# A mark ahead of GpSimd's register loads, and two loads of results issued one expert tile further ahead

## The chip, the cores and the metric

The kernel runs on one core of a Trainium2 chip. The metric is the device time of one execution in microseconds (us), as the median of several runs. A profile of one execution shows what each engine did: TensorE (PE, its weight loads PEld), VectorE (DVE), ScalarE (ACT), GpSimd (POOL) and SyncE (SP). An engine's instructions pass through its sequencer (PEq, SPq, POOLq and so on in the profile), which waits on semaphores, loads registers, takes branches and issues DMAs.

## What is computed

Four batches of 512 tokens of width 512 pass through a gated linear cross attention over a context of 1024 rows, and then through a mixture of eight experts, of which each token uses two. All is float32.

```python
def _L0_ffn_ref(x, Wr, We, be):
    logits = jnp.einsum('bsd,de->bse', x, Wr)
    w, sel = jax.lax.top_k(logits, K_TOP)
    w = jax.nn.softmax(w, axis=-1)
    gate = jnp.einsum('bsk,bske->bse', w, jax.nn.one_hot(sel, E, dtype=w.dtype))
    out = jnp.zeros(x.shape[:2] + (We.shape[2],), dtype=x.dtype)
    for e in range(E):
        out = out + gate[..., e:e + 1] * (jnp.einsum('bsd,df->bsf', x, We[e]) + be[e])
    return out
x = x + _L0_xattn_ref(_layernorm(x, axis=-1), ctx_2048, ...)
x = x + _L0_ffn_ref(_layernorm(x, axis=-1), L0_ffn_Wr, L0_ffn_We, L0_ffn_be)
return x
```

The change lies in the last stage, the mixture of experts.

## The kernel before

**Stages.** For each batch in turn the kernel forms keys and values of the context, the attention of the batch's tokens, and the router's choice of two experts for each token. `dispatch` (line 519) then scatters each token's normalized row, from GpSimd, into a DRAM buffer `stream`, which has one region for each expert. Rows of one expert are later read back in tiles of 128.

**Expert tiles.** At most 39 tiles (ALLT) of 128 rows can arise. The first 17 (EARLY) hold rows of the first three batches alone and run in between the last batch's attention. The other 22 (LATE) come after the last dispatch. 18 of these (SURE) always run; the remaining four stand in a branch, `tc.If(many > SURE)` of line 1012, which is taken only if the streams hold more tiles. In the profiled execution it isn't: there are 35 scatters of results, 17 + 18. Each engine takes this branch at its own time, and an engine that skips the body brings the semaphores of the body's work up to date.

**One expert tile** (`run`, line 677) has four parts. `rows` loads 128 rows from `stream` on SyncE (line 704), five tiles ahead. `turned` turns them on DVE (line 721), three tiles ahead. `expert` multiplies by the expert's weights on TensorE, adds the bias on DVE into y (line 753), and scatters y from GpSimd with an indirect DMA into a DRAM buffer `result` (line 757), where each choice of each token has one row.

**Token tiles.** The 16 token tiles of 128 tokens are put together again as their results become complete: `fetch` (line 810) loads both results of each token of a tile, 512 KB, from `result`; `add` (line 834) weights them and adds them to the attention's output, two instructions on DVE (line 840); `store` (line 849) writes the output, 256 KB. For token tiles 0 to 13 this is spread over the steps of the late loop (`for j in range(-5, SURE)`, line 995): `begins` (line 867) has for each token tile the step after which it is loaded. The add comes three steps later and the store one step after the add, on GpSimd's queue; from begins of SURE - 4 (14) on, adds and stores fall to step SURE, which is traced after the branch, with the stores on ScalarE's queue. Token tiles 14 and 15 are loaded after the branch, on SyncE's and ScalarE's queues (lines 1022 and 1023). They wait for all scatters of results.

**Which results a load waits for.** READ (line 46) has five groups of token tiles: 0 to 3, 4 to 7, 8 and 9, 10 and 11, 12 and 13. Each comes with the number of expert tiles that hold all of the group's results if the tokens spread well; a load waits for the scatters of these expert tiles alone. Whether the assumption holds is computed (`where_to_read`, line 800); if not, the group's load reads other rows, and the token tiles are done again at the end. The row to read from is therefore a number computed on the chip, and the first `fetch` of a group loads it into a register of GpSimd's sequencer (`nc.values_load`, line 820). Tiles 12 and 13 need the scatters of all early tiles and of late tiles 0 to 15.

**The order of instructions on an engine** is made by the framework's scheduler, from dependences and a model of the work; it may move an instruction past others that the program has ahead of it. `tc.keep_in_program_order(ins)` ties an instruction behind the one that was traced just before it on the same engine. `mark` (line 455) is a memset of one cell on GpSimd, tied in this way. It is traced ahead of each scatter of results, ahead of each load of results and ahead of each store, and these are tied as well: a mark stays behind whatever was traced before it, and the DMA behind the mark. `values_load` isn't tied. So after a group's first `fetch` the order in the program is

```
mark, scatter of the expert tile, register load, mark, load, mark, load or store ...
```

in which the mark behind the register load is tied to the register load, and not to the scatter. `tc.issue_after(latest["y"].ins)` around each step's additional work ties DVE's instructions of it behind the last y, and no other engine's.

In the late loop, the program order on GpSimd is, for step j: the scatter of late tile j (for j below 0 that of early tile 17 + j), then what `at_step[j]` holds, loads ahead of stores. Behind step 17 come the register loads for the two branches (line 1006) and the branch.

Of the kernel before, what the change touches and what calls it, by code (L numbers as in the profile page):

```python
# [39 lines left out]
SURE = LATE - 4  # L40
# [13 lines left out]
def xattn_moe_kernel(  # L54
# [388 lines left out]
    def behind(dma, puts, why):  # L443

        for put in puts:
            tc.add_manual_dep(
                dma.ins,
                put.ins.name,
                mybir.DependencyInfo(mybir.DependencyClass.Sync, mybir.DependencyReason.DATA),
                reason=why,  # L450
            )
# [3 lines left out]
    def mark():  # L455

        tc.keep_in_program_order(nc.gpsimd.memset(marked, 0.0))
# [352 lines left out]
    def fetch(t, tiles, queue, group=None):  # L810

        pool, tag = homes[t // 2 % len(homes)]
        if t not in fetched:
            pair = pool.tile([P, 2, 2, F], F32, tag=tag, name=f"y_{t}")
            fetched[t], fetched[t + 1] = pair[:, 0], pair[:, 1]
        if group is None:
            src = flat[:, t]
        else:
            if group not in rows_of:
                rows_of[group] = nc.values_load(  # L820
                    spots[0:1, group : group + 1], [queue.engine], min_val=0, max_val=NOWHERE,
                    skip_runtime_bounds_check_because="one of two constants",
                )
            row = rows_of[group] + (t - READ[group][0]) * 2 * P
            src = result[ds(row, 2 * P), :].rearrange("(p i) f -> p i f", i=2)
        mark()
        load = queue.dma_start(out=fetched[t], in_=src)
        behind(load, written["result"][:tiles], "results of the tokens")
        for put in written["result"][tiles:]:
            tc.declare_no_dep(load.ins, put.ins, reason=read_again)  # L830
        tc.keep_in_program_order(load)
        read_back.append(load)
# [31 lines left out]
    def plan(step, *what):  # L864
        at_step.setdefault(min(step, SURE), []).append(what)

    begins = (-3, -2, -1, 0, 5, 6, 7, 8, 10, 11, 14, 15, SURE - 1, SURE - 1)
    for g, (lo, hi, most) in enumerate(READ):
        for t in range(lo, hi):
            plan(begins[t], fetch, t, most, nc.gpsimd, g)  # L870
# [151 lines left out]
    for t in range(half, B * NT):  # L1022
        fetch(t, ALLT, queues[t % 2])
# [5 lines left out]
    with tc.If(again > 0):  # L1029
        for t in range(half):  # L1030
            fetch(t, ALLT, nc.sync)
            add(t, gates_end)
            store(t, nc.sync)
# [43 lines left out]
```

## Time and profile before

| what | us |
|---|---|
| median of 3 runs | 621.65 |
| lowest and highest of these | 619.83, 622.51 |
| the profiled execution, its time | 622.61 |
| its span, from first to last instruction | 621.0 |
| TensorE busy | 588.5 (95% of the span) |
| DVE busy | 271.0 (44%) |
| GpSimd busy | 100.6 (16%) |
| scatter of results, line 757, 35 of them | 35.8 in all, 1.02 each |
| issue of a load of results, line 827, GpSimd, 14 of them | 0.546 to 0.605 each |
| such a load, 512 KB, from issue to landing | 4.6 to 6.8 |
| issue of a store, line 851, GpSimd, 10 of them | 0.547 to 0.598 each |
| register load of line 820, 5 of them | 0.302, 0.311, 0.707 (least, median, most) |
| mark (memset of one cell) | 0.09 |

The granted clock of TensorE is 0.983 over the span. Moved bytes and the DMA engines' share in stretches at the end of the kernel:

| stretch, us | DMA share | GB/s |
|---|---|---|
| 570 to 580 | 0.94 | 272 |
| 580 to 590 | 0.93 | 288 |
| 590 to 600 | 0.62 | 185 |
| 600 to 607.3 | 0.63 | 218 |
| 607.3 to 613.7 | 0.81 | 229 |
| 613.7 to 621 | 0.42 | 159 |

In rows of the timeline the first number is the start in us from the start of the span, the second the length in us, then engine, line, operation and tiles (out<-in), and in brackets how long the engine was idle before and what ended this. `<-issue` stands for time in which the engine waited for nothing that the profile shows. The length of a DMA's row on GpSimd is that of its issue, not of the transfer.

### The profile page before, as it was taken

What the parts mean: (1) busy time and instruction counts of PE and PEld (TensorE: products, weight loads), DVE (VectorE), ACT (ScalarE), POOL (GpSimd) and SP (SyncE); (2) the same over time, 40 slices, a digit from 0 to 9 for tenths busy, and PEclk for the clock granted to TensorE, in tenths of its full rate; (3) what the DMA queues carried; (4) which work ended last, traced back from release to release, by engine and by line L of the source; (5) the groups of instructions that cost most, each with busy time, mean ns of one, the idle gap of its engine ahead of it and who ended that gap; (6) DMA issues with size and microseconds to landing.
All of it is one profiled execution on the core that took longest, in us unless ns stands there. A gap on an engine that the chain in (4) does not pass through costs nothing. (4 is left out here: it accounts for less than half of the span.)

```text
span 621.0 us, 6578 instructions
## 1 busy us (share of the span) xinstructions
PE 588.5 (95%) x1908; PEld 286.3 (46%) x1908; DVE 271.0 (44%) x668; ACT 115.2 (19%) x180; POOL 100.6 (16%) x274
## 2 busy tenths in 40 slices
PE   7999999999999999999999999999999999999940
PEld 3555543454565335446643454565434554443410
DVE  2222243216215341351454226127874569475663
ACT  1322222112322221142222211322210100000000
POOL 4100000000002200000050000002311227455540
PEclk9999999999999999999999999999999999999985
DMA  8648920682686227527530660933344444889965
GB/s 317 191 158 301 293 81 2 167 240 69 164 248 184 81 86 237 153 85 221 186 137 1 203 204 0 327 130 137 116 114 119 96 119 177 262 243 259 296 219 173
DMA packets 68597, 105.55 MB, mean 170 GB/s; under 512 B 11981, under 2 KB 30413, under 8 KB 68176
## 3 DMA queue, kind: packets, MB, share of 16 engines
q1 hardware_dynamic: 58944, 76.24, 41.7%
q0 software_dynamic: 8176, 26.78, 12.1%
q10 hardware_dynamic: 1440, 2.10, 1.1%
q8 instruction: 16, 0.26, 0.2%
q14 instruction: 21, 0.17, 0.1%
HBM read 45.93 MB, written 59.94 MB: 170 GB/s over the span
## 5 line engine op out<-in xcount | busy, mean ns | idle before, releaser
L91 PE MATMUL pk<-wkv_sb,cT 128*128 128x512 f32 x256 | 118.6, 607 | 4.4 <-DMA cT<-in_cT_dram 4.4
L91 PE MATMUL pv<-wkv_sb,cT 128*128 128x512 f32 x256 | 115.2, 593 | 0.0
L221 DVE TENSOR_SCALAR ex<-pk 128x512 f32<-128x512 f32 x32 | 22.0, 688 | 148.3 <-PE pk L91 148.3
L91 PEld LDWEIGHTS pv<-wkv_sb,cT 128*128 128x128 f32 x256 | 48.4, 190 | 62.3 <-issue 59.3
L91 PEld LDWEIGHTS pk<-wkv_sb,cT 128*128 128x128 f32 x256 | 47.7, 194 | 57.8 <-issue 49.9
L91 PE MATMUL pe<-we_sb,xgT 128*128 x144 | 62.8, 595 | 0.6 <-DVE xgT L721 0.6
L91 PE MATMUL pe<-we_sb,turned_rows 128*128 x136 | 60.3, 597 | 0.7 <-DVE turned_rows L721 0.7
L278 POOL MEMSET v<- 128x4 f32 x32 | 3.3, 105 | 345.3 <-PE kvs L91 282.3
L91 PE MATMUL pg<-xT,wg_sb 128*128 128x512 f32 x128 | 56.7, 596 | 0.0
L91 PE MATMUL pq<-xT,wq_sb 128*128 128x512 f32 x128 | 56.6, 596 | 0.0
L91 PE MATMUL po<-wo_sb,aT 128*128 128x512 f32 x128 | 55.6, 592 | 0.0
L222 ACT ACTIVATE ex<-ex 128x512 f32<-128x512 f32 x48 | 30.2, 630 | 136.2 <-DVE ex L221 126.6
L757 POOL DMA_INDIRECT result<-y,to x35 | 35.8, 1023 | 93.7 <-DVE y L753 88.4
L91 PEld LDWEIGHTS pe<-we_sb,xgT 128*128 128x128 f32 x144 | 27.0, 190 | 36.3 <-issue 29.9
L91 PEld LDWEIGHTS pe<-we_sb,turned_rows 128*128 128x128 f32 x136 | 25.3, 190 | 32.4 <-issue 29.5
L563 POOL DMA_INDIRECT stream<-row,slot x32 | 31.9, 996 | 50.3 <-DVE cmp L591 22.5
L91 PEld LDWEIGHTS kvs<-v,k 128*128 128x128 f32 x256 | 33.3, 191 | 13.4 <-issue 13.4
L91 PEld LDWEIGHTS pg<-xT,wg_sb 128*128 128x128 f32 x128 | 24.0, 190 | 32.1 <-issue 32.1
L91 PEld LDWEIGHTS po<-wo_sb,aT 128*128 128x128 f32 x128 | 24.1, 190 | 29.2 <-issue 28.7
L91 PEld LDWEIGHTS pq<-xT,wq_sb 128*128 128x128 f32 x128 | 23.8, 190 | 27.3 <-issue 27.3
L91 PE MATMUL kvs<-v,k 128*128 128x129 f32 x256 | 34.0, 275 | 0.0
L223 DVE SCALAR_TENSOR_TENSOR k<-pk,ex 128x512 f32<-128x512 f32 x32 | 22.1, 690 | 19.5 <-ACT ex L222 19.5
(175 smaller groups left out, 465.1 us busy)
## 6 DMA issues: line engine op xcount, KB each, us to landing
stream<-empty SPq DMA_DIRECT2D x24, 1028.0 KB, 8.1
stream<-empty SPq DMA_DIRECT2D x8, 1285.0 KB, 6.8
xg<-stream SPq DMA_DIRECT2D x140, 64.0 KB, 2.7
we_sb<-in_we_dram SPq DMA_DIRECT2D x32, 256.0 KB, 5.5
cT<-in_cT_dram SPq DMA_DIRECT2D x31, 256.0 KB, 3.1
y<-result POOLq DMA_DIRECT2D x14, 512.0 KB, 5.5
x<-in_x_dram SPq DMA_DIRECT2D x16, 256.0 KB, 6.6
out_dram<-y POOLq DMA_DIRECT2D x10, 256.0 KB, 4.6
```

The costliest lines, as they stand in the source:

```text
L91: tc.keep_in_program_order(nc.tensor.matmul(**operands))
L221: nc.vector.tensor_scalar(ex, src, 0.0, None, ALU.min)
L222: nc.scalar.activation(ex, ex, AF.Exp)
L223: nc.vector.scalar_tensor_tensor(dst, src, 0.0, ex, ALU.max, ALU.add)
L278: nc.gpsimd.memset(v[:, :, P : P + 1], 1.0)
L563: put = nc.gpsimd.indirect_dma_start(out=stream, out_offset=bass.IndirectOffsetOnAxis(ap=slots[i][:, t, :], axis=0), in_=rows[t], in_offse ...
L757: put = nc.gpsimd.indirect_dma_start(out=result, out_offset=bass.IndirectOffsetOnAxis(ap=home_i, axis=0), in_=y, in_offset=None, bounds_ch ...
```

## The change

Two lines. In `fetch`, a mark is traced ahead of the register load of a group. It applies to the five groups, whose first loads stand in steps -3, 5, 10, 14 and, for tiles 12 and 13, the step of the second edit. In `begins`, token tiles 12 and 13 move from step SURE - 1 (17) to step SURE - 2 (16).

```diff
             if group not in rows_of:
+                mark()
                 rows_of[group] = nc.values_load(
                     spots[0:1, group : group + 1], [queue.engine], min_val=0, max_val=NOWHERE,
                     skip_runtime_bounds_check_because="one of two constants",
...
-    begins = (-3, -2, -1, 0, 5, 6, 7, 8, 10, 11, 14, 15, SURE - 1, SURE - 1)
+    begins = (-3, -2, -1, 0, 5, 6, 7, 8, 10, 11, 14, 15, SURE - 2, SURE - 2)
```

The new mark is tied behind the scatter of the step's expert tile, since this is what was traced just before it on GpSimd. Adds and stores of token tiles 12 and 13 stay at step SURE, behind the branch.

## The prediction

> **What bounds the kernel now.** I read the page first, then the chain that ended last, then GpSimd's rows of the last 30 us, and at the end DVE's rows and the branch's own rows. TensorE is busy 95% of the span, but the change touches only GpSimd's queue, so what counts is where that queue decides something. The chain shows one such place, the end:
>
> ```profile
> 590.10 0.56 POOL y L827
> 590.66 0.08 POOL marked L457
> 590.74 1.28 issue
> 592.02 11.38 DMA out_dram<-y
> 603.41 0.09 POOLq L1012
> ...
> 604.72 2.33 DMA result<-y,to
> ...
> 607.30 6.38 DMA y<-result
> ```
>
> Each row is start, length and what it was. TensorE's last matmul ends at 597.3. From there the kernel waits for one scatter, that of late tile 17: it starts at 604.72, lands 2.33 later, and only then do SyncE and ScalarE load the results of token tiles 14 and 15 (6.38). The adds and stores behind that end the span at 621.0. GpSimd's rows say why the scatter is so late:
>
> ```profile
> 592.88 1.02 POOL L757 DMA_INDIRECT result<-y,to  x1 [0.23 <-issue]
> 595.60 1.02 POOL L757 DMA_INDIRECT result<-y,to  x1 [1.70 <-DVE y L753]
> ...
> 598.18 1.02 POOL L757 DMA_INDIRECT result<-y,to  x1 [0.27 <-DVEq L1012]
> 599.18 0.23 POOL L457 MEMSET marked<- 1x1 f32 x2
> 600.06 0.56 POOL L827 DMA_DIRECT2D y<-result  x1 [0.64 <-issue]
> 600.62 0.09 POOL L457 MEMSET marked<- 1x1 f32 x1
> 600.71 0.55 POOL L827 DMA_DIRECT2D y<-result  x1
> 604.72 1.03 POOL L757 DMA_INDIRECT result<-y,to  x1 [3.46 <-issue]
> ```
>
> The indirect DMAs are the scatters of tiles 14, 15, 16 and 17, the direct ones the loads of token tiles 12 and 13. In the program tile 17's scatter stands ahead of both loads; here it comes after them, and after more. Its input was long there, and GpSimd did something else in between:
>
> ```profile
> 597.35 0.69 DVE L753 TENSOR_TENSOR y<-pe,be_sb 128x512 f32<-128x512 f32 x1 [1.21 <-PE pe L91]
> 598.38 0.18 DVE L1003 COPY gates_end<-gates 128x32 f32<-128x32 f32 x1 [0.34 <-DVEq L1012]
> ```
>
> ```profile
> L1012 POOLq COMPARE_BRANCH   x1: 53/53/53, 601.1 to 601.1; - x1
> L1012 POOLq INC_SWDGE_SEM  x1: 2002/2002/2002, 601.5 to 601.5; - x1
> ```
>
> Tile 17's y is done at 598.04. GpSimd takes the branch of line 1012 at 601.1 and spends 2.00 us in a semaphore update that belongs to the skipped body, and the scatter follows. So it slipped past the register loads, the two loads and the whole branch. The same happened to the copy into gates_end on DVE, which the program also has ahead of the branch. The slips have a rule: a scatter stays in place only where the next mark is traced right behind it. Where a register load is, the next mark is tied to that load. Five scatters had such a place (early tile 14, late tiles 5, 10, 14, 17), and all five slipped.
>
> **The change, part by part.** Late tile j's scatter is s(j), token tile t's load f(t).
>
> *Five more marks.* Each memset is 0.09 us. They tie s to the line: s, new mark, register load, mark, f. That the second mark stays behind the first follows from both writing one cell. So in four places s goes ahead of f, and f waits for DVE's y.
>
> - Group 0: y of early tile 14 ends at 529.01. Scatters start 0.28 after their y (585.97 to 586.25), so at 529.3 instead of 531.43. f(0): 529.3 + 1.02 scatter + 0.24 for two marks + 0.64 to issue (as at 589.23 to 590.10) = 531.2 instead of 530.54. It lands by 536 and is added at 542.83.
> - Group 1: y(5) ends at 557.31; s(5) 557.6 instead of 559.52; f(4) 559.5 instead of 558.65. It landed at 564.1, now 565.0; added at 570.67.
> - Group 2: y(10) ends at 576.56; s(10) 576.8 instead of 577.11; f(8) 578.7 instead of 575.63. With 4.6 to 6.8 to land (the row of these loads) 583.3 to 585.5; added at 590.20.
> - Group 3: y(14) ends at 592.32; s(14) 592.6 instead of 592.88; f(10) 594.5 instead of 590.10, behind it the store of tile 8 at 595.1, then s(15) at 594.5 + 1.48 (f, store, scatter as at 575.63, 576.26, 577.11) = 596.0 instead of 595.60. **Term: +0.4 us for everything behind it on GpSimd.** f(10) lands near 599.8, its add stood at 599.60: the cover is used up, 0.2 us late. That is absorbed, since the adds of tiles 10 to 13 end near 608 and DVE then idles until 613.7 for tile 14.
>
> In the first three I cost the later load at nothing: 7, 5.7 and 4.7 us lie between landing and add. Without that cover DVE would stand by the delay, 0.7 to 3.1 us, and y and TensorE behind it.
>
> *Tiles 12 and 13 a step ahead.* They need the scatters up to s(15), in both orders. Their order on GpSimd is s(16), mark, register load, mark, f(12), mark, f(13): the very order of the trace of before, with one mark of another origin. So f(12) and f(13) do not come earlier, but 0.4 later: 600.44 and 601.09, landing at 605.0 and 606.3. The mark of tile 17 now stands behind f(13), at 601.6.
>
> *What becomes of s(17)?* The shift has taken the last register load of fetch from behind it. What is traced next are the register loads of line 1006 and the branch, and neither has a mark in front. So s(17) is as free as before to slip past the branch. Nothing in the trace shows this order, so both ends are to be priced.
>
> Below: it slips again. f(13), branch, 2.00 us update, s(17), all 0.4 later: 605.1, loads at 607.7, the span 621.0 + 0.4 = 621.4. Above: it stays ahead of the branch. s(17) starts 0.31 after tile 17's mark (576.80 to 577.11), at 601.95. Landing 2.33 later is 604.3. But the final loads wait for the skipped body's semaphores too: ScalarE's and SyncE's waits moved on only when that update was over. From the end of f(13) (601.26) to its end (603.50) was 2.24; behind s(17) that makes 601.95 + 1.03 + 2.24 = 605.2, and with the 0.26 between the last release and the load (607.04 to 607.30) 605.5 instead of 607.30, a gain of 1.8.
>
> I take the first. In group 2 GpSimd ran through four DMAs (s(9), a store, f(8), a store) and a further mark before the scheduler saw y(10) ready; between y(16) and y(17) there are now only three and the mark. And gates_end on DVE shows that the branch was placed before y(17) was over. **Sum: +0.4 us** (bounds 0, if y(15) hides the delay, and +0.9, with a register load of 0.71, the longest of line 820, in place of 0.31).
>
> The profiled execution took 622.61 with a span of 621.0; the median is 621.65 (619.83 to 622.51), 0.96 lower. I put the difference on the median: 621.65 + 0.4 = 622.05, said as 622.1.
>
> The Trainium skill ("TensorE: Matmul & The Clock Gate", the table at its head) calls GpSimd's queue strictly first in, first out. This speaks against the change: a load that is tied behind a scatter can't pass it while the scatter waits for DVE. The rows agree, no f starts while an s ahead of it waits; if loads could pass, the +0.4 would be 0.
>
> The skill also gives a register load a floor of about 600 ns ("DMA: Bandwidth & Descriptors", Latency and other measured facts). The rows of line 820 have 302 at least and 311 in the middle, so the measurement decides. By the page the two loads of groups 3 and 4 would add some 0.6 us (an estimate), a median of 622.6.
>
> **The rivals.**
>
> *s(17) stays ahead of the branch.* For it: tile 17's mark is now behind f(13), and the branch's own marks come behind that one; if y(17) is ready by then, the scatter is first in the program. Against: five slips of five. Time: 621.65 - 1.8 = 619.8. If the 2.00 us update overlaps the scatter, the loads start at 604.3 + 0.26, a gain of 2.7; and if they land in the 5.5 of the other loads instead of 6.38, because two of the four stores beside them come later, 3.6: 618.1.
>
> *Loads collide with tile rows (the slower side).* f(8) and the store behind it, 768 KB, move 3.1 us, into the stretch 580 to 590 where the DMA share is 0.93 at 288 GB/s and three weight loads already idled 0.75, 0.55 and 0.66 us for late rows instead of the usual 0.24, 1.24 too long together. 768 KB at 288 GB/s are 2.7 us. All of it on the rows' path gives 0.4 + 2.7 = 3.1, 624.8. It decides from the point where those three gaps grow by more than the 1.8 that the rival above could save, and shows as slower only if all of it arrives. Against it: the sum of the DMA work is unchanged, and the same bytes leave the stretch before. The mirror image is worth the 1.24 of the gaps.
>
> *The marks do not hold.* If two writes of one cell are no tie for the scheduler, s(16) slips behind f(12) and f(13), which wait for s(15)'s landing (598.24). GpSimd's work is the same, only permuted, up to the branch: 621.7.
>
> **How the numbers follow.** Slips again 0.47, stays ahead 0.33, collision 0.13, marks do not hold 0.07. A measurement of this kernel tells about 0.5% from no change, 3.1 us: below 618.5 or above 624.8. Under 618.5 lie the better half of the second case and a little of a mirrored collision: 0.20. Above 624.8 lie the worse part of the collision and what I have not seen: 0.13. Within: 0.67. The forecast's own range is 621.6 to 622.6. The range of 8 in 10 runs from the second case's end to just below the collision at full price: 618.1 to 624.5.
>
> **What would show it.** Right: in GpSimd's rows s(17) still follows the branch and the 2.00 us update, near 605; s(5), s(10), s(14) stand ahead of f(4), f(8), f(10); f(10) near 594.5; the adds of tile 10 wait a little. Wrong: two scatters with only the two loads between them and the branch behind, the final loads near 605.5; or DVE idle for y<-result ahead of an add before 598, or TensorE's last matmul off 597.3 by over 1 us.

## The result, and the profile after

The changed kernel takes 622.57 us (median of 20 runs, 621.02 to 624.17), the kernel before in the same runs 621.11 (20 runs, 619.41 to 624.33). The ratio is 1.0028, with a 95% interval of 1.0018 to 1.0037: slower by 0.3%, 1.5 to 1.7 us, inside the 0.5% that were called no change. Measured again on another chip it was 623.30 against 622.47, 1.0024 [1.0006, 1.0043].

The profiled execution of the changed kernel took 621.79, with a span of 620.2 and a granted clock of 0.982. That one execution is shorter than the profiled one of before (span 621.0), because late tile 17's y was ready at 596.32 and not at 598.04; what follows y is longer. So places in the two traces are compared below by their distance from an event ahead of all that changed at the end: the end of y(14), 592.33 before and 590.60 after.

GpSimd's rows of the changed kernel (start, length, engine, line, operation, tiles, and in brackets the idle time before with what ended it):

```profile
590.89 1.01 POOL L757 DMA_INDIRECT result<-y,to  x1 [3.86 <-DVE y L753]
...
592.73 0.59 POOL L828 DMA_DIRECT2D y<-result  x1 [0.61 <-issue]
...
593.33 0.58 POOL L852 DMA_DIRECT2D out_dram<-y  x1
...
594.27 1.02 POOL L757 DMA_INDIRECT result<-y,to  x1 [0.30 <-DVE y L753]
...
595.32 0.55 POOL L828 DMA_DIRECT2D y<-result  x1
...
596.83 1.02 POOL L757 DMA_INDIRECT result<-y,to  x1 [0.29 <-issue]
...
599.16 0.56 POOL L828 DMA_DIRECT2D y<-result  x1 [1.10 <-DMA result<-y,to]
...
599.82 0.55 POOL L828 DMA_DIRECT2D y<-result  x1
...
600.70 1.02 POOL L757 DMA_INDIRECT result<-y,to  x1 [0.25 <-issue]
```

The direct loads are f(10), f(11), f(12), f(13), the scatters s(14) to s(17). Two things are to be seen. The scatter of tile 14 now stands ahead of f(10), so f(10) and the store behind it come just ahead of s(15); and f(12) waits 1.10 for a scatter's landing, where in the trace of before it had waited for nothing shown. And s(17), the last row, comes straight behind f(13), ahead of the branch: it is no longer behind the 2.0 us semaphore update. That update follows it (rows of the branch's line, with least, median and most ns and the start):

```profile
L1013 POOLq INC_SWDGE_SEM  x1: 2017/2017/2017, 601.8 to 601.8; - x1
```

All the same the final loads came no sooner. The rows of the scatters' line in a window that holds s(17) alone give its time to land:

```profile
L757 POOL DMA_INDIRECT result<-y,to x1: 1023/1023/1023, 600.7 to 600.7; - x1
...
DMA to landing us min/median/max: 5.4/5.4/5.4
```

5.41 us, where it took 2.33 before. It lands at 606.11. The update ended at 603.85, and the rows of the final loads on their queues show that SyncE then stood in one event wait of 2253 ns, from 603.88 to 606.13, right up to that landing:

```profile
L828 SPq EVENT_SEMAPHORE  x4: 28/28/2253, 603.9 to 606.3; - x4
```

So the sum at the end, all from rows: s(17) starts 12.39 behind the end of y(14) before, 10.09 after, 2.30 earlier; it lands 3.08 slower; the final loads stand at 14.93 before and 15.72 after, 0.79 later. The end of the span moves from 28.69 to 29.61.

Two rows of DVE answer to the copy into gates_end that had slipped behind the branch:

```profile
596.24 0.20 DVE L1004 COPY gates_end<-gates 128x32 f32<-128x32 f32 x1
597.32 0.75 DVE L841 SCALAR_TENSOR_TENSOR y<-y,gates_end,x 128x512 f32<-128x512 f32 x1 [0.88 <-DMA y<-result]
```

It stays ahead of the branch now too, and the first add of token tile 10 waits 0.88 for f(10).

### The profile page after: what moved, and what is told of

Its sections match the earlier page's. It is cut to its first block, busy times and chain, and to the rows that moved or that the text cites. A ratio compares the mean times of both kernels' runs of the same rounds, so it can differ in the third digit from the quotient of the medians.

```text
span 620.2 us, 6584 instructions
## 1 busy us (share of the span) xinstructions
PE 587.0 (95%) x1908; PEld 286.1 (46%) x1908; DVE 271.1 (44%) x668; ACT 115.2 (19%) x180; POOL 100.6 (16%) x279
## 5 line engine op out<-in xcount | busy, mean ns | idle before, releaser
L91 PEld LDWEIGHTS kvs<-v,k 128*128 128x128 f32 x256 | 33.3, 191 | 13.4 <-issue 13.4
L753 DVE TENSOR_TENSOR y<-pe,be_sb 128x512 f32<-128x512 f32 x35 | 24.0, 687 | 15.8 <-PE pe L91 13.3
```

The costliest lines, as they stand in the source:

```text
L91: tc.keep_in_program_order(nc.tensor.matmul(**operands))
L753: latest["y"] = nc.vector.tensor_tensor(y, pe, be_sb[:, ds(no, 1), :].rearrange("p o f -> p (o f)"), ALU.add)
```

## The experiments

Twelve runs were made, on several chips and each beside the kernel before on the same chip: nine new kernels, one of them twice, and both kernels of the change once more. Three theories stood against each other. **Queue:** the loss arises in GpSimd's queue at the end, from group 3's mark (f(10) ahead of s(15)), and s(17)'s gain is eaten because its data lie behind two loads. **Early marks:** the marks of groups 0 to 2 cost the time. **Collision:** loads moved into stretches where they delay TensorE's rows.

All results in one table. "Marks" names the groups with a mark ahead of their register load, "shift" the move of tiles 12 and 13. The four columns behind the ratio are from the profiled execution, us behind the end of y(14): the start of f(12), of s(17), of the first of the two final loads, and the end of the span.

| kernel | marks | shift | ratio to before [95%] | f(12) | s(17) | final load | end |
|---|---|---|---|---|---|---|---|
| before | none | no | 1 | 7.73 | 12.39 | 14.93 | 28.69 |
| before_again | none | no | 0.9994 [0.9979, 1.0010] | 7.74 | 12.40 | 14.99 | 28.82 |
| after | 0-4 | yes | 1.0028 [1.0018, 1.0037] | 8.56 | 10.09 | 15.72 | 29.61 |
| after_again | 0-4 | yes | 1.0024 [1.0006, 1.0043] | 8.53 | 10.07 | 15.67 | 29.43 |
| early_groups | 0-2 | no | 1.0009 [0.9994, 1.0024] | 7.77 | 12.44 | 14.98 | 28.77 |
| group3 | 3 | no | 1.0027 [1.0011, 1.0043] | 8.33 | 13.78 | 16.33 | 30.12 |
| first_groups | 0-3 | no | 1.0027 [1.0009, 1.0045] | 8.59 | 13.65 | 16.18 | 29.98 |
| shift_only | none | yes | 0.9987 [0.9971, 1.0002] | 6.66 | 9.46 | 14.57 | 27.94 |
| last_group | 4 | yes | 0.9988 [0.9971, 1.0006] | 7.73 | 9.28 | 14.37 | 28.17 |
| no_group3 | 0-2, 4 | yes | 1.0016 [1.0000, 1.0031] | 11.54 | 13.07 | 17.99 | 31.84 |
| last_mark | 4 | no | 0.9982 [0.9958, 1.0006] | 9.19 | 7.00 | 13.26 | 24.91 |
| last_mark_again | 4 | no | 0.9971 [0.9945, 0.9998] | 9.47 | 7.16 | 13.54 | 25.15 |
| mark_only | 0-4 | no | 1.0001 [0.9972, 1.0029] | 9.91 | 7.69 | 13.99 | 26.19 |
| act_loads | see below | no | 0.9992 [0.9974, 1.0010] | 6.18 | 7.00 | 13.08 | 26.70 |

**Each edit alone: mark_only and shift_only.**

```diff
             if group not in rows_of:
+                mark()
```

> The five marks without the shift: order at the end s(16), s(17), f(12), f(13), branch. Queue theory (what GpSimd's queue transfers, it transfers in the order of issue, so a scatter behind two loads of 512 KB lands with them; and the skipped branch's 2.0 us update comes after): s(17) starts 1.3 after y(17) ends and lands within 4.4 of its start; the final loads start about 7 us after y(17) ends instead of 9.25 (before) and 10.05 (changed), so 0.995 to 0.999 of before. Collision theory (loads that come later in the stretch 575 to 595 hold up tile rows and TensorE): the marks of groups 0 to 3 are in it, so 1.002 to 1.004 as in the changed kernel, or at best half of that.

The five marks alone gave 621.55 against 622.05, but the times fall into two groups: six at 618.35 to 620.24, six at 622.86 to 626.64. The profiled execution belongs to the lower one: its final loads start 7.07 behind the end of y(17), as the queue theory said, but the median did not fall. The granted clock is 0.985 to 0.988 for the lower six and 0.983 to 0.985 for the others. In each trace it is 1.0 from about 10 us on until 2 to 6 us behind TensorE's last matmul, and 0.5 from there on, so a longer end alone would lower it; the cause of the two groups is open.

```diff
-    begins = (-3, -2, -1, 0, 5, 6, 7, 8, 10, 11, 14, 15, SURE - 1, SURE - 1)
+    begins = (-3, -2, -1, 0, 5, 6, 7, 8, 10, 11, 14, 15, SURE - 2, SURE - 2)
```

> The kernel before with the second edit alone: tiles 12 and 13 a step ahead, no new mark. The program then has on GpSimd: s(15), a mark, the register load of group 4, f(12), s(16), f(13), s(17), and only then the branch. Queue theory (group 3's mark makes the loss, s(17) behind two loads makes the gain small): nothing changes up to s(15), f(10) stands ahead of s(14) and starts near 590; s(17) starts ahead of the branch's 2.0 us update, at 599 to 601, lands 4 to 5.5 later behind f(12) and f(13); the final loads stand 7.0 to 8.5 behind the end of y(17) instead of 9.2; ratio 0.997 to 1.000, as for the shift with the last mark (0.9988). Rival: the shift has a cost of its own, because f(12) and f(13) now lie in the queue around s(16) and ahead of s(17): then this run is as slow as the changed kernel with group 3's mark taken out, 1.001 to 1.003, with the final loads 9 or more behind y(17).

621.93 against 622.77. GpSimd's rows of this kernel:

```profile
596.92 0.54 POOL L827 DMA_DIRECT2D y<-result  x1 [0.92 <-DMA result<-y,to]
597.76 1.02 POOL L757 DMA_INDIRECT result<-y,to  x1 [0.30 <-DVE y L753]
...
598.80 0.57 POOL L827 DMA_DIRECT2D y<-result  x1
...
599.73 1.48 POOL L757 DMA_INDIRECT result<-y,to  x1 [0.28 <-DVE y L840]
```

s(16), with the register load right behind it, slips behind f(12). s(17) stands behind f(13), as in the program, and stays ahead of the branch with none of the new marks: the shift does that alone. The final loads start 7.10 behind the end of y(17). The rival, a cost of the shift itself (1.001 to 1.003), falls; the interval of the ratio just takes in 1, so the gain of some 0.8 us is likely and not certain.

**Which marks cost: group3, first_groups, early_groups.**

```diff
             if group not in rows_of:
+                if group == 3:
+                    mark()
```

> Before with the mark of group 3 alone. Theory G3: the whole loss of the run with the first four marks, 1.002 to 1.004 of before; f(11) lands about 7.5 us after y(15) ends instead of 6.0, the skipped branch's update ends 7 us after y(17) ends instead of 5.5, final loads 10 to 10.5 instead of 9.25. Rival G012: 0.999 to 1.001.

One mark makes the loss of the whole change: 624.12 against 622.47. GpSimd's rows of it:

```profile
595.22 1.02 POOL L757 DMA_INDIRECT result<-y,to  x1 [0.29 <-DVE y L753]
...
596.26 0.56 POOL L829 DMA_DIRECT2D y<-result  x1
...
599.88 0.57 POOL L829 DMA_DIRECT2D y<-result  x1 [0.86 <-DMA result<-y,to]
...
600.53 0.55 POOL L829 DMA_DIRECT2D y<-result  x1
605.33 1.03 POOL L757 DMA_INDIRECT result<-y,to  x1 [4.25 <-DMA y<-result]
```

Here s(17) does slip behind the branch, and its 4.25 of idle time were ended by a load's landing. The rows of the branch's line say how:

```profile
L1014 POOLq EVENT_SEMAPHORE  x3: 17/17/43, 601.1 to 602.3; - x3
L1014 POOLq COMPARE_BRANCH  x1: 53/53/53, 600.9 to 600.9; - x1
L1014 POOLq INC_SWDGE_SEM  x1: 2002/2002/2002, 602.4 to 602.4; - x1
```

The branch is taken at 600.9, but the update starts at 602.42, behind three event waits, of which the last starts at 602.3. f(11)'s last semaphore event in the trace is at 602.31. So the skip waits for earlier DMAs of the queue to land, then spends its 2.00, and s(17) follows. In the trace of before f(11) landed at 601.35 and the update began at 601.50.

```diff
+                if group < GROUPS - 1:
+                    mark()
```

> Marks of groups 0 to 3 alone, no shift: s(17) slips behind the branch as before, f(8) and f(10) go later as in the changed kernel. Queue theory: the end is before's plus at most 0.5, so 1.000 to 1.001. Collision theory: the whole of the slowdown, 1.002 to 1.004, with y(17) later against y(0) by 1 us or more.

The marks of groups 0 to 3: 623.92 against 622.05, the same loss, and s(17) slips as well. The time is what the collision theory said and more than the queue theory's 1.000 to 1.001, but in its trace y(17) comes no later against y(0) than before (55.78 us and 55.91) and the end comes 1.2 later behind y(14): the place is the queue theory's, its price of 0.5 at most was too low.

```diff
+                if group < 3:
+                    mark()
```

> Before with the marks of groups 0 to 2 alone; f(10) and the end are as before. If the loss lies in group 3's mark alone: 0.999 to 1.001, final loads 9 to 9.6 us after y(17) ends. If f(8)'s later issue also costs, by holding up tile rows: 1.001 to 1.003, with TensorE's weight loads idle for rows by 2 us or more between 560 and 580 and final loads still 9 to 9.6 after y(17).

623.40 against 622.17. The end of the trace is that of before to 0.1 us (14.98, 28.77). What the marks of groups 0 to 2 cost alone is at most 0.24%, and may be nothing.

**Without group 3's mark: last_group and no_group3.** Both have the second edit of the change, and the mark under a condition:

```diff
+                if group == GROUPS - 1:
+                    mark()
```

> The shift with the mark of the last group alone; groups 0 to 3 as before, so f(10) goes early again. Queue theory: s(17) still stands behind f(12) and f(13), lands 4.5 to 5.5 after its start, final loads 9.5 to 10 after y(17) ends: 1.000 to 1.002 of before. Collision theory: nothing moves before step 16, so TensorE ends as before: 0.999 to 1.001.

621.73 against 622.05. With f(10) ahead of s(14) again, f(12) is back at 7.73 and s(17) at 9.28; it lands 4.88 later by the trace's semaphore events. The final loads start 7.28 behind the end of y(17), not 9.5 to 10 as the queue theory had said, and the time doesn't tell it from the collision theory's 0.999 to 1.001.

```diff
+                if group != 3:
+                    mark()
```

> The changed kernel without the mark of group 3 (tiles 10 and 11), so f(10) again goes ahead of s(14). Theory G3 (the price is that mark: f(10) and the store behind it come 2.6 to 4.4 us later and into GpSimd's queue ahead of s(15) and f(11), whose landings f(12) and the skipped branch's update wait for): like the run with the last group's mark and the shift, 0.997 to 1.000 of before, final loads 7 to 8.5 us after y(17) ends. Rival G012 (the marks of groups 0 to 2): no better than the changed kernel, 1.002 to 1.004, final loads about 10 us after y(17).

622.81 against 622.47: it should have been as fast as last_group, and wasn't. Its profiled execution, 625.21, shows a late row instead. A row each of DVE, of TensorE's weight loads and of GpSimd, from their timelines:

```profile
595.23 0.71 DVE L721 STREAM_TRANSPOSE xgT<-xg 128x512 f32<-128x512 f32 x1 [3.45 <-SPq L1014]
```

```profile
596.00 0.30 PEld L91 LDWEIGHTS pe<-we_sb,xgT 128*128 128x128 f32 x2 [1.01 <-DVE xgT L721]
```

```profile
598.85 1.02 POOL L757 DMA_INDIRECT result<-y,to  x1 [5.42 <-DVE y L753]
```

The last tile's rows landed so late that DVE stood 3.45 before it could turn them; TensorE stood 1.01; y(15) and s(15) came 3.8 behind their place in the trace of before (the releaser named is SyncE's skip of the branch, whose semaphore events end with the rows' landing). That is the collision, in one execution, one of the three slowest of twelve. That it makes the 0.16% of this kernel's runs isn't shown, since only one was profiled.

**The last mark without the shift: last_mark.**

```diff
+                if group == GROUPS - 1:
+                    mark()
```

> The last group's mark alone, no shift: s(16), s(17), then f(12) and f(13), then the branch; groups 0 to 3 as before. Theory G3: no part of the loss, s(17) lands ahead of the two loads, final loads 6.5 to 7.5 us after y(17) ends: 0.994 to 0.998. If the mark and not the shift brings what is to be had at the end, it is faster than the run that had mark and shift (0.9988). Rival (the end is bound by the DMA engines' work and not by who waits for whom): 0.998 to 1.000.

> The last group's mark alone, once more, since its times were spread over 617.5 to 625.2: together with the first run 0.996 to 1.000 of before. A second profile: s(17) ahead of f(12) and f(13), and the span ends 19 to 21 us after y(17) ends if the first profile was of the program; 22 or more if the gain at the end is there in some executions only.

621.53 against 622.47, and 620.44 against 622.17: the only version whose interval stays below 1, and that in the second measurement alone. Its medians lie 0.2 to 0.3% below the kernel before and further below the changed one. GpSimd's rows of the second, s(16) to f(13):

```profile
596.64 1.02 POOL L757 DMA_INDIRECT result<-y,to  x1 [0.28 <-issue]
...
597.97 1.48 POOL L757 DMA_INDIRECT result<-y,to  x1 [0.22 <-issue]
...
600.28 0.58 POOL L829 DMA_DIRECT2D y<-result  x1 [0.64 <-issue]
...
600.94 0.57 POOL L829 DMA_DIRECT2D y<-result  x1
```

s(17) is ahead of both loads now, not behind them, and by the semaphore events it lands at 601.29, 3.3 after its start. What the final loads wait for is now the update, which starts at 602.04 and ends at 604.06; the first stands at 604.35. ScalarE's queue stood in one event wait of 2996 ns, from 601.05 to 604.05, and SyncE's next waits are all short:

```profile
L829 ACTq EVENT_SEMAPHORE  x7: 38/38/2996, 601.0 to 604.5; - x7
L829 SPq EVENT_SEMAPHORE  x5: 27/28/28, 604.0 to 604.3; - x5
```

The profile's chain names f(12)'s landing at 604.19 instead, but in the trace of mark_only the first final load starts at 604.57 and f(12) lands at 605.17, so these loads don't wait for it.

**The two loads on another queue: act_loads.** To take them out of GpSimd's queue altogether, they go to ScalarE's, and a mark ahead of line 1006 ties s(17) ahead of the branch:

```diff
-            plan(begins[t], fetch, t, most, nc.gpsimd, g)
+            plan(begins[t], fetch, t, most, nc.scalar if g == GROUPS - 1 else nc.gpsimd, g)
...
+    mark()
     many, again = (
```

> Before, with token tiles 12 and 13 loaded from ScalarE's queue and a mark ahead of the register loads of the branch: s(16), s(17), branch with no load between. Queue theory: s(17) starts 0.3 to 1.3 after y(17) ends, lands within 3.5, the 2.0 us update ends 3.6 to 4.5 after y(17) ends, final loads 4.5 to 5.5 after it instead of 9.25: 0.992 to 0.995 of before. Collision theory says nothing of the end; if the end doesn't follow the scatter, 0.999 to 1.001.

621.24 against 622.05, far from the 0.992 to 0.995 that the queue theory had said. The final loads come 1.85 earlier than before (13.08), 7.4 behind the end of y(17) and not 4.5 to 5.5. The rows of ScalarE's two loads, of s(17), and of the final loads' waits:

```profile
598.23 0.91 ACTq L827 DMA_DIRECT2D y<-result  x2
```

```profile
599.06 1.27 POOL L757 DMA_INDIRECT result<-y,to  x1 [0.22 <-issue]
```

```profile
L827 ACTq EVENT_SEMAPHORE  x5: 38/38/1303, 603.5 to 603.8; - x5
```

The last load ahead of s(17) in GpSimd's queue is f(11) now, as in last_mark, and s(17) starts at the same 7.00 as there; yet by its semaphore events it lands at 605.07, 6.01 after its start, against 3.33 in last_mark. ScalarE stood in one event wait of 1303 ns up to that landing, and its final load starts at 605.13. SyncE's, at 605.49, comes behind its skip of the branch, which waits for ScalarE's two loads (landed at 603.28 and 604.73). So the two loads slow a scatter that follows them from another queue too: the order within GpSimd's queue is not what makes it late, but that the loads are in flight.

**Both kernels again.**

> The changed kernel once more, beside the others on one chip: 1.002 to 1.004 of before. Its profile is the second of this program: if the 10.05 us from y(17) to the final loads is of the program and not of one execution, they start 9.7 to 10.5 us after y(17) ends.

> The kernel of before against itself: 0.998 to 1.002. It gives a second profile of before: if the 9.25 us from y(17) to the final loads is of the program, they start 9.0 to 9.6 us after it, and the span ends 22.5 to 23.5 us after y(17) ends.

The change's loss holds, and before against itself gives 0.9994 [0.9979, 1.0010], which is how finely 12 runs tell.

**What the table shows together.** Against the kernel before (28.69 and 28.82), the end is later by 1.2 to 1.4 with group 3's mark alone or with groups 0 to 3, by 0.8 with the whole change, not at all with groups 0 to 2, and earlier by 0.6 to 0.8 with the shift without early marks. The timed differences are +1.7, +1.5 to +1.7, +0.6 and -0.8. So what happens at the end gives the signs of these and most of their sizes, but only half of the whole change's 1.5 to 1.7; where the other half arises isn't shown. Against last_group, which has the shift and the last mark as well, the changed kernel's end is 1.44 later: the early marks cost with the shift what group 3's mark costs without it. The end doesn't give no_group3 (+1.0), nor the three kernels whose profiled executions end 2.0 to 3.8 earlier while their medians gain 0 to 1.8: last_mark's 24 times spread from 616.6 to 625.2, and the profiled executions were among the four fastest of each twelve. That their slower executions have late rows, as no_group3's profile had, is only argued.

## Why the prediction was right or wrong

The time, 622.1, was 0.5 off, and no change within 0.5% was called likeliest; the way there was wrong, and the nearness was partly luck. The change was put at +0.4 and cost 1.5 to 1.7, on a kernel before that measured 621.11 and not 621.65; s(17) gained 2.30 at its start that the sum didn't have, and lost 3.08 in landing that it didn't have either.

**"s(17) slips again"** is the step that failed: "I take the first", under *What becomes of s(17)?*. s(17) stayed ahead of the branch. "Five slips of five" was read as a rule about the mark behind a scatter, yet all five had a register load of `fetch` traced right behind them; behind s(17) of the changed kernel stand only those of the branch. In the four kernels with the shift s(17) stays; in the four with neither the shift nor the last mark (before, early_groups, group3, first_groups) it slips. Why the scheduler lets it pass the one kind of register load and not the other isn't shown.

**The rival that had the order right had the wrong price.** *s(17) stays ahead of the branch* was to gain 1.8, with a landing of 2.33. It started 10.09 behind y(14), 0.46 later than costed (601.95 - 592.32 = 9.63) and still 2.30 earlier than before, but the landing was 5.41. The row of 2.33 belonged to a scatter that went out 4.0 behind the last load's issue; now it lies 0.88 behind f(13) and 1.54 behind f(12), 512 KB each, which landed at 605.39 and 604.06. last_mark is the counterproof: ahead of both loads, 3.3 (4.25 in mark_only, where f(10) and f(11) are later too). That it is the loads, and not their place in GpSimd's queue, act_loads shows with 6.01.

The Trainium skill ("DMA: Bandwidth & Descriptors", SWDGE vs HWDGE vs iDMA) says that only one queue context is allocated for the DMAs that GpSimd issues. The scatter that lands behind the loads issued ahead of it agrees with that, but doesn't prove it: in act_loads, where the loads are ScalarE's, it landed behind them as well. The page's fit for one such DMA (Anatomy of one DMA) would give 2.6 us for the scatter's 256 KB, an estimate, near the 2.33 measured well behind the loads and far from the 5.41 measured just behind them.

**"+0.4 us for everything behind it on GpSimd"** was right where it was worked out and too small where it ended. s(15) moved from 3.27 to 3.67 behind y(14), by 0.40 (3.84 in after_again, where y(15) itself came later); f(10) stood at 2.12 (2.2 was said). But only the issue was costed, not the landing. Behind f(10) and its store, s(15) took 4.21 to land instead of 2.65, so f(12) waited 1.10 instead of 0.64 and stood 0.83 later. In the same way f(11) landed at 10.47 instead of 9.03, and where s(17) slips, the skip waits for that (group3): 1.4 later at the final loads, not 0.4. Had s(17) slipped as predicted, the end would by that row have come 1.4 later.

**Marks.** They hold: s(5), s(10) and s(14) stand ahead of f(4), f(8), f(10), and the rival *marks do not hold* fell. Costing the later loads of groups 0 to 2 at nothing agrees with early_groups' trace; up to 0.24% of the time is left open.

**Collision** didn't carry the result. From the end of y(4) to that of y(17) the two traces of before took 42.5 and 42.3, those of the changed kernel 43.5 and 42.5, and group 3's mark alone made a loss of this size (42.8). It exists as a single event (no_group3).

**"That is absorbed"**, of tile 10's add: it waited 0.88, and DVE idled 6.24 ahead of tile 14's add, so it was.

## What to carry to other kernels

Price a DMA that you move by what is in flight at its new place, from whatever queue: its landing, and the landings of what now stands behind it, not its issue, and not the landing it had in its old place. Here a scatter on the path that sets the end belonged ahead of the bulk loads, not just ahead of the branch, and it didn't help to give the loads to another queue. And a skipped branch isn't free: its semaphore bookkeeping waits for earlier DMAs to land and holds back what is queued behind it.

## What the hardware showed unexpectedly

- Skipping a body with GpSimd's DMAs cost 1.98 to 2.02 us in one semaphore update in every trace, and in group3 and before this began only 0.11 and 0.15 behind f(11)'s landing, in the changed kernel 0.11 behind that of the store which follows f(11).
- s(17), a scatter of 256 KB, landed in 2.32 to 2.37 us when issued 4.0 to 4.8 behind f(13), in 3.3 or 4.25 when 2.2 to 2.3 ahead of the two loads, in 4.7 to 5.4 just behind them, in 6.01 when they were ScalarE's. In the changed kernel it went out into a stretch with a DMA share of 0.87 (600 to 604), in the trace of before into one with 0.26 (604 to 608).
- s(15)'s and f(11)'s landing events in the changed kernel come in two parts: 13 of 16 by 597.70 and by 600.01, the other three at 598.4 to 598.5 and from 601.02. What waits for all 16 waits up to a microsecond for three.
- The same two final loads and four stores ran at different rates. From the first final load's start to the end of the span it took 13.8 in before and 11.6 in last_mark_again. The windows from 608 to 612 of the two, with the clock, DMA share and GB/s at the end of the line:

```profile
608.00:612.00 4.00, 0.00 (x0) 0.00 (x0) 0.00 (x0) 0.00 (x0) 0.00 (x0) 0.50 0.91 224
```

```profile
608.00:612.00 4.00, 0.00 (x0) 0.00 (x0) 2.92 (x4) 0.00 (x0) 0.00 (x0) 0.50 0.96 362
```

The share is nearly the same, the rate is 1.6 times as high. In the first ScalarE's load starts 0.04 ahead of SyncE's, in the second SyncE's is 0.19 ahead and f(13) is still landing. The three traces with SyncE's load ahead (last_mark twice, mark_only) took 11.6 to 12.2, the eleven others 13.4 to 13.9. In all three f(13) was still landing, so which of the two matters isn't shown.
